# A cross-attention kernel: the context turned by VectorE, its keys and values made in four row tiles

## The chip, the cores and the metric

The kernel runs on one core of a Trainium2 chip. The metric is the device time of one execution in microseconds (us). The time before is the median of three runs.

## The reference

Two transformer layers on x (4 batches, 512 tokens, 320 channels), all in float32. Each layer is self-attention, cross-attention to a context (4 batches, 1601 tokens, 192 channels), and a gated feed-forward block with inner width 1280, each behind a layer norm and with a residual. Attention has 20 heads of 16 channels.

```python
h1 = _ln(x, n1_g, n1_b)
x = _attn(h1, h1, q1, k1, v1, o1_w, o1_b, heads) + x
h2 = _ln(x, n2_g, n2_b)
x = _attn(h2, context, q2, k2, v2, o2_w, o2_b, heads) + x
h3 = _ln(x, n3_g, n3_b)
a, g = jnp.split(h3 @ ff_w1 + ff_b1, 2, axis=-1)
x = a * gelu(g) @ ff_w2 + ff_b2 + x
```

`_attn` is softmax(q k^T / 4) v per head, then a projection. The same context serves both layers, with different weights.

## The kernel before

**Units and rounds.** The work is cut into units: for each layer, first self-attention, then cross-attention, over 4 batches and 5 groups of 4 heads (20 units each), then 4 feed-forward units. An attention unit (`main`, L883) walks over chunks of 128 keys: 4 chunks in self-attention, 13 in cross-attention, where the last one holds 65 keys. One chunk is a round. In a round TensorE makes the transposed scores of the chunk for the 4 heads (`st`, L891), ScalarE takes their exponentials (`pr`, L897), and one round later TensorE multiplies these with the values (`av`, L911). ScalarE copies `av` to `vo` (L927) and GpSimd adds it to the output (L928). Beside the scores of the current unit, TensorE computes the scores of the next unit the other way round (`sps`, L730 and L745), only for VectorE to find each query's maximum (L738, L755). The maxima are turned and sent by small DMAs on SP's queue into spare rows of q (`max_end`, L781), so that the score product itself subtracts them.

**Tiles of the array.** A head has 16 channels, so its q and k lie in a slot of 32 partitions, and a score product uses 32 rows of the array; two `st` and two `sps` products in different rows run together. `av` uses all 128 rows and 32 columns for each head. The projections for queries (`qps`, L601), keys (`kps`, L626), values (`vps`, L678) and output (`ops`, L839) have 96 to 128 rows and 32 columns, four products in different columns. Every product is in float32.

**Steps.** All the rest is done in steps, which stand in chains (L273): context, norm, queries and keys ("proj" and "early"), values, project, divide. `steps` (L343) is called once in a round, after the `av` product. It takes steps whose due time is next while a credit allows; the credit grows each round by what all queued steps cost over the time until they are due (`pace`, L321). Steps that cost nearly nothing (`LIGHT`, L276) are run two in a round. `until` (L368) runs a chain at once when its result is needed. The order of all instructions is thus fixed when the program is built.

**Banks.** There are eight PSUM banks in two rings of four: `ps_st` for `st` and `av`, `ps_m` for `sps`. A step takes one bank of `ps_m` (`step_bank`, L283).

**The context.** For each batch the context is loaded in pairs of chunks (`load_context`, L474) and turned on TensorE in seven steps (`turn`, L504): products with an identity matrix of up to 128 x 96 into one bank (`cps`, L514), copied by ScalarE (L518) to `ctxT`, which holds 96 partitions x 2 x 1601. The result is saved to memory for the second layer (L523), which loads it instead of turning it (L496). There is one `ctxT` buffer, which the feed-forward block uses too.

**Keys and values.** The keys of a group are made in four steps (`keys`, L621) of about 2 x 200 tokens: 2 parts of 96 channels x 4 products. ScalarE copies the bank to `kst`, and GpSimd spreads it over the slots of `kT` (`to_slots`, L541, L556: four instructions for a step). `kwhen` notes when each step's keys are there, and maxima of columns that are complete may start three half rounds later (`at_hand`, L1104). The values are made a chunk at a time (`values`, L669), in two parts of 8 and 12 heads (128 and 192 columns), and copied by ScalarE to `vals` (L686).

**Weights.** The deque `loads` is emptied by one entry in each attention unit. `load_cross` (L193) loads the weights of cross-attention, `load_ff` (L199) those of the feed-forward block, w1 in two DMAs of 1280 KB.

Of the kernel before, what the change touches and what calls it, by code (L numbers as in the profile page):

```python
# [36 lines left out]
CK = [(0, 0, 96), (1, 96, 96)]  # L37
NHC = FF // P
# [21 lines left out]
def kernel(ctx: ExitStack, tc: tile.TileContext, x, context, ws, out):  # L60
# [83 lines left out]
    wk2, wv2 = (wpool.tile([P, 2, D], F32, name=n) for n in ("wk2", "wv2"))  # L144
    w1 = wpool.tile([P, 2, 2 * FF], F32, name="w1")

# [46 lines left out]
    def load_cross(l):  # L193
        load_norm(l, 1)
        load_rows(wq2, ws[l]["q2"], DK)
        load_rows(wk2, ws[l]["k2"], CK)
        load_rows(wv2, ws[l]["v2"], CK)

    def load_ff(l):  # L199
# [11 lines left out]
        for k in FK:  # L211
            loads.append(lambda k=k: load_rows(w1, ws[l]["ff_w1"], [k]))
# [3 lines left out]


    class Unit:


        def __init__(self, l, kind, b, g):
            self.l, self.kind, self.b, self.g = l, kind, b, g
            self.cross = kind == "cross"
            self.nkeys = S2 if self.cross else N
            self.nch = (self.nkeys + P - 1) // P
            self.kck = CK if self.cross else DK

            s = slices(self.nkeys, 8 if self.cross else 2)
            self.kpairs = [s[i : i + 2] for i in range(0, len(s), 2)]
            self.kmade = 0  # L230
            self.kwhen = []
            self.vmade = [0, 0]
            self.made = {"q": 0, "k": 0}
            self.scored = 0
            self.valued = 0
            self.steps = 2 * self.nch if kind != "ff" else 2 * NHC + NQ
            self.before = self.other = None
            self.early = False
            self.own = {}
            self.pairs = self.hT = self.q = self.kvT = None  # L240
# [32 lines left out]
    chains = {n: deque() for n in ("divide", "project", "norm", "context", "early", "proj", "values")}  # L273
    clock = {"round": 0, "credit": 0.0, "lights": 0, "tiles": None}
# [68 lines left out]
    def steps(beside, lights=1):  # L343
# [3 lines left out]
        clock["lights"] = lights  # L347
        clock["tiles"] = True if beside is None else None
        done = 0
        while True:  # L350
# [13 lines left out]
            if cost == LIGHT:  # L364
                clock["lights"] -= 1
        clock["tiles"] = None
# [107 lines left out]
    def load_context(b, i):  # L474
# [9 lines left out]
        if rows % P:  # L484
            dma(out=t[: rows % P, full, :], in_=context[b, (c0 + full) * P : S2, :])
        ctx_in[b, i] = t


    saved = [dram.tile([CK[0][2], 2, S2], F32, name=f"ctxT{b}") for b in range(B)]

    def add_context(l, b, put, due, free):
        s = {}

        def load():
            s["cT"] = one.tile([P, 2, S2], F32, tag="ctxT", name="ctxT")
            dma(out=s["cT"][: CK[0][2]], in_=saved[b])  # L496
            s["round"] = clock["round"]

        if l:
            add("context", 0.0, load, due - 14, free)  # L500
            add("context", 0.0, lambda: put(s["cT"]), due - 2, yes, lambda: clock["round"] >= s["round"] + 8)
            return

        def turn(i):  # L504
            if i == 0:
                s["cT"] = one.tile([P, 2, S2], F32, tag="ctxT", name="ctxT")
            c0, n = CGRP[i]
            t = ctx_in.pop((b, i))
            rows = min(S2, (c0 + n) * P) - c0 * P
            ps = step_bank([P, 2, 2 * P], "cps")  # L510
            for k, at, w in CK:
                for c in range(n):
                    r = min(P, rows - c * P)
                    nc.tensor.transpose(  # L514
                        ps[:w, k, c * P : c * P + r], t[:r, c, at : at + w], ident[:r, :r]
                    )
            w = CK[0][2]
            nc.scalar.copy(s["cT"][:w, :, c0 * P : c0 * P + rows], ps[:w, :, :rows])  # L518
            if i + 2 < len(CGRP):
                load_context(b, i + 2)  # L520
            if i + 1 == len(CGRP):
                put(s["cT"])
                dma(out=saved[b], in_=s["cT"][:w])  # L523

        for i in range(len(CGRP)):
            add("context", 0.58, lambda i=i: turn(i), due - 2 * (len(CGRP) - i), free if i == 0 else yes)
# [31 lines left out]
    def add_proj(u):  # L558
        wq, wk = (wq2, wk2) if u.cross else (wq1, wk1)
        chain = "early" if u.early else "proj"  # L560

        due = lead(u) - 6

# [10 lines left out]
        if u.g == 0:  # L574
            last = units[u.before.i - u.before.g] if u.before else None

            def free():

                return last is None or last.made["k"] == G and last.vmade[1] == last.nch

            if u.cross and not u.early:
                add_context(u.l, u.b, lambda t: u.own.update(kv=t), due - 4, free)

            def hold():
                until(lambda: "h" in u.own, "norm")
                if u.cross:
                    until(lambda: "kv" in u.own, "context")
                u.hT = u.own["h"]
                u.kvT = u.own.get("kv", u.own["h"])

            add(chain, 0.0, hold, due - 4, yes, lambda: "h" in u.own and (not u.cross or "kv" in u.own))
# [29 lines left out]
        def keys(pair):  # L621
            ps = step_bank([P, 512], "kps")
            for k, at, n in u.kck:
                for i, to, gs in tiles:
                    c0, w = pair[i]
# [3 lines left out]
                        rhs=first.kvT[:n, k, c0 : c0 + w],  # L629
                        start=(k == 0),  # L630
                        stop=(k == len(u.kck) - 1),
                    )
            if u.i:
                stage = two.tile([P, N // 2], F32, tag="stage", name="kst")
                wide = min(w for _, w in pair)
                nc.scalar.copy(stage[:, :wide], ps[:, :wide])  # L636
            for i, (c0, w) in enumerate(pair):
                if u.i == 0:
                    to_slots(u.kT, u.k0 + c0, ps, w, i, True, keep)
                    continue  # L640
                if w > wide:
                    rows = slice(i * GD, (i + 1) * GD)
                    nc.scalar.copy(stage[rows, wide:w], ps[rows, wide:w])  # L643
                to_slots(u.kT, u.k0 + c0, stage, w, i, True)
            u.kmade += 1
            u.kwhen.append(-9 if start["on"] else clock["round"])
            first.made["k"] += u.kmade == len(u.kpairs)
# [5 lines left out]
        for part in range(parts):  # L653
            add(chain, (0.05 + 0.427 / parts,) * 3, lambda part=part: queries(part), due - 2, unread)
        for pair in u.kpairs:
            c0, w = pair[-1]
            chunks = (c0 + w + P - 1) // P

            def free(chunks=chunks):

                return u.other is None or u.other.scored >= min(chunks, u.other.nch)

            add(chain, (0.15 / len(u.kck) + w / 600,) * len(u.kck), lambda pair=pair: keys(pair), due + (c0 - w) // 300, free)

    def add_values(u):

        wv = wv2 if u.cross else wv1

        def values(i, cs):  # L669
# [3 lines left out]
            for c in cs:  # L673
                r = min(P, u.nkeys - c * P)
                at = (c - cs[0]) * w
                for k, _, n in u.kck:
                    for f, m in tiles_of(r):
                        nc.tensor.matmul(  # L678
                            ps[f : f + m, at : at + w],
                            lhsT=u.kvT[:n, k, c * P + f : c * P + f + m],  # L680
                            rhs=wv[:n, k, h0 * DH : h1 * DH],
                            start=(k == 0),
                            stop=(k == len(u.kck) - 1),
                        )
            m = len(cs)
            nc.scalar.copy(  # L686
                vals[:r, cs[0] : cs[0] + m, h0:h1, 0:DH],
                ps[:r, : m * w].rearrange("p (c h d) -> p c h d", c=m, d=DH),
            )
            u.vmade[i] += m  # L690

        for i, g in enumerate((0, 2)):
# [3 lines left out]
            whole = u.nkeys // P  # L696
            sets = [range(c, c + 1) for c in range(whole)]
            if u.nkeys % P:
                sets.append(range(whole, whole + 1))
            for cs in sets:  # L700

                def free(c=cs[-1], user=user):
                    return u.kvT is not None and (user is None or user.valued > min(c, user.nch - 1))

                add(
                    "values", (0.15 + w / 600 * len(u.kck),) * len(cs), lambda i=i, cs=cs: values(i, cs),
                    units[u.i + g].start + 2 * cs[0], free,
# [3 lines left out]
    def max_pairs(u):  # L711
# [7 lines left out]
        def have(end):  # L719
            assert keys_of(u) >= end  # L720

# [5 lines left out]
        def full_one(t, s, j):  # L727
            have((s + 1) * 512)
# [11 lines left out]
        def rest_two(heads):  # L740
            have(u.nkeys)
# [141 lines left out]
    def main(u, give, nxt):  # L883
# [3 lines left out]
        def score(c, j, pool=ps_st, tag="st"):  # L887
# [4 lines left out]
                st[:r, :], lhsT=u.kT[rows, u.k0 + c * P : u.k0 + c * P + r], rhs=u.q[rows, :], start=True, stop=True  # L892
# [172 lines left out]
    def before(u):  # L1065

        if u.kind == "cross" and u.g == 1 and u.b + 1 < B or u.kind == "self" and u.m == EARLY - 2:
            b = u.b + 1 if u.cross else 0
            if u.l == 0:
                load_context(b, 0)  # L1070
                load_context(b, 1)
        if u.kind == "self" and u.m == EARLY:

            add_context(u.l, 0, lambda t: units[u.i - u.m + B * G].own.update(kv=t), u.start + 36, yes)

    def after(u):

        stage[u.b] += 1
        if u.b == B - 1:
# [5 lines left out]
            if u.l + 1 < L:  # L1085
                if u.kind == "ff":
                    load_ff(u.l + 1)
                else:
                    load = load_self if u.kind == "self" else load_cross
                    loads.append(lambda: load(u.l + 1))  # L1090
# [4 lines left out]
    def columns(v, pairs):  # L1095

        full = v.nkeys // 512
        s = (full * NQ + bool(v.nkeys % 512) - len(pairs)) // NQ
        return min(v.nkeys, (s + 1) * 512)

    def keys_of(v):
# [143 lines left out]
```

## Time and profile before

| what | value |
|---|---|
| median of 3 runs | 3273.88 us (3269.45 to 3275.33) |
| the profiled execution, its own time | 3271.09 us |
| its span, first to last instruction | 3269.3 us |
| mean granted TensorE clock | 0.996 |
| TensorE, context keys (L626, 96 rows), busy | 135.7 us + 34.4 us for two forms, beside each other |
| VectorE, 512-column maxima (L738), 2560 of them, busy | 1591 us |
| ScalarE, exponentials (L897), busy | 1411.0 us |
| GpSimd, additions of `vo` (L928), 1277 ns each | 735.7 us |
| SP's DMA queue | 47.92 MB, 5.5% of 16 engines' span |

Busy time of a group is the time in which at least one of its instructions runs, so that the times of groups that run together must not be added. A float32 product stands as two records in the profile (two passes). A group's mean is that of one record with its latency, and is longer than the time from one start to the next. The timeline merges neighbouring instructions of one form into a line with its count.

### The profile page before, as it was taken

The page shows a single profiled execution, that of the slowest core. Times are in us where ns is not written, and L with a number is a line of the kernel's source. Part 1 is how long each engine was busy: PE and PEld are TensorE (multiplying, and loading weights), DVE is VectorE, ACT ScalarE, POOL GpSimd, SP SyncE. Part 2 cuts the span into 40 slices and gives each one's busy share as a digit, 9 for nine tenths or more (in the row PEclk, how much of TensorE's full clock was granted, in tenths as well). Part 3 has the DMA queues.
Part 4 walks back from the last instruction along what each step waited for, and adds up shares of the span by engine and source line. Part 5 has one row for each costly group of instructions (what it writes and reads, how often), then busy time and mean ns, then how long its engine had stood idle before and what let it go on. Part 6 is the DMA issues. An engine that isn't in the chain of part 4 may idle for free.

```text
span 3269.3 us, 82086 instructions
## 1 busy us (share of the span) xinstructions
PE 3221.7 (99%) x33554; PEld 1455.4 (45%) x33554; DVE 2090.6 (64%) x3844; ACT 2029.1 (62%) x4191; POOL 1525.4 (47%) x2254
## 2 busy tenths in 40 slices
PE   9999999999999999999999999999999999999999
PEld 4444444344444444355444444444444444443555
DVE  7777777677777777522248777777777777774221
ACT  4666467777877877711136665678778778775110
POOL 4545456556655655210224554566556556642000
PEclk9999999999999999999999999999999999999999
DMA  1210000100100000000002100000000000000000
GB/s 52 73 40 24 9 12 10 45 9 5 30 10 6 28 5 4 8 1 0 1 21 61 33 10 7 7 22 8 5 19 5 5 20 4 5 5 4 9 11 14
DMA packets 48844, 53.17 MB, mean 16 GB/s; under 512 B 23372, under 2 KB 41812, under 8 KB 47188
## 3 DMA queue, kind: packets, MB, share of 16 engines
q1 hardware_dynamic: 48384, 47.92, 5.5%
q8 instruction: 265, 4.34, 0.5%
q14 instruction: 111, 0.91, 0.1%
q0 software_dynamic: 64, 0.00, 0.0%
q10 hardware_dynamic: 20, 0.00, 0.0%
HBM read 29.21 MB, written 7.54 MB: 11 GB/s over the span
## 4 chain that ended last, share of the span: by engine, by line
PE 89%; DVE 5%; POOL 3%; issue 1%; ACT 1%; DMA 1%; SPq 1%; DVEq 0%; POOLq 0%; ACTq 0%
PE st L891 22%; PE av L911 19%; PE sps L730 15%; PE fps L1014 9%; PE yps L1049 5%; PE kps L626 4%; PE vps L678 4%; PE ops L839 3%; PE qps L601 3%; DVE nmax L738 2%; PE fps L1026 2%; PE sps L745 1%; PE hps L434 1%; DVE pm L738 1%; POOL kT L556 1%
## 5 line engine op out<-in xcount | busy, mean ns | idle before, releaser
L897 ACT ACTIVATE pr<-st 128x512 f32<-128x512 f32 (+1 forms) x2720 | 1411.0, 602 | 545.8 <-PE sps L730 425.8
L738 DVE TENSOR_REDUCE pm<-sps 128x1 f32<-128x512 f32 x1920 | 1195.1, 682 | 423.7 <-PE sps L730 420.9
L891 PE MATMUL st<-q,kT 32*128 32x512 f32 (+1 forms) x5440 | 1368.1, 617 | 21.7 <-ACT pr L897 6.9
L730 PE MATMUL sps<-kT,q 32*128 32x512 f32 x5120 | 1285.9, 620 | 3.8 <-ACT kst L643 2.4
L928 POOL TENSOR_TENSOR o<-o,vo 128x512 f32<-128x512 f32 x576 | 735.7, 1277 | 1048.1 <-ACT vo L927 882.1
L911 PE MATMUL av<-pr,vals 128*32 128x512 f32 (+1 forms) x5440 | 732.2, 607 | 4.8 <-ACT pr L897 4.8
L891 PEld LDWEIGHTS st<-q,kT 32*128 32x128 f32 (+1 forms) x5440 | 467.9, 181 | 333.6 <-ACT pr L897 160.4
L730 PEld LDWEIGHTS sps<-kT,q 32*128 32x128 f32 x5120 | 442.3, 184 | 231.6 <-issue 152.6
L738 DVE TENSOR_REDUCE nmax<-sps 128x1 f32<-128x512 f32 x640 | 395.9, 680 | 153.4 <-PE sps L730 151.8
L556 POOL TENSOR_SCALAR kT<-kst,keep,ones 64x200 f32<-64x200 f32 (+2 forms) x796 | 413.8, 520 | 80.0 <-ACT kst L636 22.3
L927 ACT COPY vo<-av 128x512 f32<-128x512 f32 x576 | 350.5, 609 | 19.9 <-PE av L911 19.2
L911 PEld LDWEIGHTS av<-pr,vals 128*32 128x32 f32 (+1 forms) x5440 | 110.1, 108 | 502.4 <-ACT pr L897 482.4
L1032 ACT ACTIVATE gl<-fps,b 128x512 f32<-128x512 f32 x80 | 54.8, 687 | 376.9 <-PE fps L1026 376.8
L1014 PE MATMUL fps<-hT,w 128*128 128x512 f32 x640 | 288.0, 599 | 0.0
L556 POOL TENSOR_SCALAR q<-qst,keep,zero 64x128 f32<-64x128 f32 (+1 forms) x476 | 229.8, 483 | 89.8 <-ACT qst L613 58.9
L1014 PEld LDWEIGHTS fps<-hT,w 128*128 128x128 f32 x640 | 117.4, 190 | 147.6 <-issue 141.9
L678 PEld LDWEIGHTS vps<-wv,ctxT 96*32 96x32 f32 (+1 forms) x3264 | 102.8, 109 | 108.0 <-issue 88.8
L678 PE MATMUL vps<-wv,ctxT 96*32 96x192 f32 (+2 forms) x3264 | 148.2, 299 | 0.0
L382 POOL TENSOR_SCALAR root<-root 128x4 f32<-128x4 f32 x23 | 5.3, 229 | 298.5 <-DVE root L376 297.9
L626 PE MATMUL kps<-ctxT,wk 96*32 96x200 f32 (+1 forms) x2560 | 135.9, 332 | 0.0
L1033 DVE SCALAR_TENSOR_TENSOR hid<-fps,b,gl 128x512 f32<-128x512 f32 x48 | 35.8, 750 | 152.5 <-ACT gl L1032 150.3
L601 PE MATMUL qps<-hT,wq 112*32 112x128 f32 (+3 forms) x2880 | 127.5, 309 | 4.3 <-DVE nmax L738 2.5
(79 smaller groups left out, 2244.2 us busy)
## 6 DMA issues: line engine op xcount, KB each, us to landing
aT<-o SPq DMA_DIRECT2D x320, 32.0 KB
q<-turned SPq DMA_DIRECT2D x636, 1.0 KB
ctxT<-ctxT SPq DMA_DIRECT2D x8, 1200.8 KB
w<-in_L_xattn_ff_w_dram SPq DMA_DIRECT2D x4, 1280.0 KB
ctxin<-in_ctx_dram SPq DMA_DIRECT2D x24, 192.0 KB
w<-in_L_xattn_ff_w_dram SPq DMA_DIRECT2D x4, 800.0 KB
out_dram<-x SPq DMA_DIRECT2D x16, 160.0 KB
x<-in_x_dram SPq DMA_DIRECT2D x3, 640.0 KB
```

What stands on the lines that cost most here:

```text
L556: nc.gpsimd.tensor_scalar(to, stage[rows, :w], keep[b][rows], more[rows], ALU.mult, ALU.add)
L601: nc.tensor.matmul(ps[to, :w], lhsT=wq[:n, k, gs], rhs=first.hT[:n, k, at[i] : at[i] + w], start=(k == 0), stop=(k == 2),)
L626: nc.tensor.matmul(ps[to, :w], lhsT=wk[:n, k, gs], rhs=first.kvT[:n, k, c0 : c0 + w], start=(k == 0), stop=(k == len(u.kck) - 1),)
L678: nc.tensor.matmul(ps[f : f + m, at : at + w], lhsT=u.kvT[:n, k, c * P + f : c * P + f + m], rhs=wv[:n, k, h0 * DH : h1 * DH], start=(k == 0),
L730: nc.tensor.matmul(ps, lhsT=u.q[j * SLOT : (j + 1) * SLOT, t * P : (t + 1) * P], rhs=u.kT[j * SLOT : (j + 1) * SLOT, u.k0 + s * 512 : u.k0 ...
L738: return lambda: nc.vector.tensor_reduce(to, ps, AX.X, ALU.max, negate=(ns == 1))
L891: nc.tensor.matmul(st[:r, :], lhsT=u.kT[rows, u.k0 + c * P : u.k0 + c * P + r], rhs=u.q[rows, :], start=True, stop=True)
L897: nc.scalar.activation(p[:r], st[:r], AF.Exp)
L911: nc.tensor.matmul(ps[i * SLOT : (i + 1) * SLOT, :], lhsT=columns_of[:r, head : head + SLOT], rhs=pr.pop((c, j))[:r, :], start=True, stop= ...
L927: nc.scalar.copy(vo, ps)
L928: nc.gpsimd.tensor_tensor(u.o, u.o, vo, ALU.add)
L1014: nc.tensor.matmul(ps, lhsT=w1[:, k, i * FF + c * P : i * FF + (c + 1) * P], rhs=u.hT[:, k, :], start=(k == 0), stop=False,)
```

## The change

The context is no longer turned as a whole. VectorE transposes it in blocks of 32 x 32: token t of chunk c lands on partition group t // 32, at column c x 32 + t % 32, with the 192 channels as 6 blocks of 32 on the 32 partitions. `ctxT` becomes 128 partitions x 6 x 416. So each of the four groups of 32 partitions holds its 32 tokens of every chunk, and the weights of keys and values are loaded four times, once for each group (`wk_q`, `wv_q`, in the space of w1, whose own load moves to the last unit of cross-attention). The last 65 tokens are turned on TensorE as well, for their values (`tail`).

A group's keys are made in one step: 6 channel blocks x 4 row groups x 2 halves of the columns, each product 32 rows x 64 columns of the array with 192 (or up to 224) moving columns, into four banks, two of each ring. ScalarE and VectorE copy two banks each; eight pieces then go to the slots, at most two in a round, in a chain of their own. The keys are due ten half rounds earlier, and maxima wait until all keys of the unit are there. In `kT` the columns now stand by row group (`cols`). Values are made for four chunks in one step: 6 channel blocks x 4 row groups, each product 32 rows x 128 columns. Self-attention keeps its steps.

```diff
+KB = CTX // 32
+QT = (NC2 - 1) * 32
+TAIL = S2 - 4 * QT
+HALF = QT // 2
...
+    w1_flat = w1.rearrange("p k f -> p (k f)")
+    wk_q, wv_q = (
+        w1_flat[:, i * KB * D : (i + 1) * KB * D].rearrange("p (k d) -> p k d", d=D) for i in range(2)
+    )
...
     def load_cross(l):
         load_norm(l, 1)
         load_rows(wq2, ws[l]["q2"], DK)
-        load_rows(wk2, ws[l]["k2"], CK)
         load_rows(wv2, ws[l]["v2"], CK)
+        for t, n in ((wk_q, "k2"), (wv_q, "v2")):
+            for i in range(4):
+                dma(out=t[i * 32 : (i + 1) * 32], in_=ws[l][n].rearrange("(k p) d -> p k d", p=32))
...
+    def load_first(l):
+
+        load_rows(w1, ws[l]["ff_w1"], FK)
...
-            ps = step_bank([P, 2, 2 * P], "cps")
-            for k, at, w in CK:
-                for c in range(n):
-                    r = min(P, rows - c * P)
-                    nc.tensor.transpose(
-                        ps[:w, k, c * P : c * P + r], t[:r, c, at : at + w], ident[:r, :r]
-                    )
-            w = CK[0][2]
-            nc.scalar.copy(s["cT"][:w, :, c0 * P : c0 * P + rows], ps[:w, :, :rows])
+            t, _ = ctx_in.pop((b, i))
+            for c in range(n):
+                at = (c0 + c) * 32
+                nc.vector.transpose(s["cT"][:, :, at : at + 32], t[:, c, :])
...
+        def tail():
+            ps = step_bank([P, 2, P], "cps")
+            for k, at, w in CK:
+                nc.tensor.transpose(ps[:w, k, :TAIL], s["last"][:TAIL, 0, at : at + w], ident[:TAIL, :TAIL])
+            w = CK[0][2]
+            nc.scalar.copy(s["tail"], ps[:w, :, :TAIL])
+            dma(out=saved_tail[b], in_=s["tail"])
+            put(s)
...
         for i in range(len(CGRP)):
-            add("context", 0.58, lambda i=i: turn(i), due - 2 * (len(CGRP) - i), free if i == 0 else yes)
+            add(
+                "context", LIGHT, lambda i=i: turn(i), due - 2 * (len(CGRP) - i), free if i == 0 else yes,
+                lambda i=i: clock["round"] >= ctx_in[b, i][1] + 3,
+            )
+        add("context", 0.3, tail, due)
...
+        keys_due = due - 10 if u.cross else due
...
+        def keys_of_context():
+
+            pss = quarter_banks("kps")
+
+            more = [max(0, min(32, TAIL - a * 32)) for a in range(4)]
+            for k in range(KB):
+                for a, ps in enumerate(pss):
+                    rows = slice(a * SLOT, (a + 1) * SLOT)
+                    for i in range(2):
+                        w = HALF + i * more[a]
+                        nc.tensor.matmul(
+                            ps[i * GD : (i + 1) * GD, :w],
+                            lhsT=wk_q[rows, k, u.g * GD : (u.g + 1) * GD],
+                            rhs=first.kvT[rows, k, i * HALF : i * HALF + w],
+                            start=(k == 0),
+                            stop=(k == KB - 1),
+                        )
+            stage = one.tile([P, 4, HALF + 32], F32, tag="kstage", name="kst4")
+            for a, ps in enumerate(pss):
+                copy = nc.vector.tensor_copy if a % 2 else nc.scalar.copy
+                copy(stage[:, a, :HALF], ps[:, :HALF])
+                if more[a]:
+                    copy(stage[GD:, a, HALF : HALF + more[a]], ps[GD:, HALF : HALF + more[a]])
+            for a in range(4):
+                for i in range(2):
+                    def piece(a=a, i=i):
+                        to_slots(u.kT, a * QT + i * HALF, stage[:, a, :], HALF, i, True)
+                        if i and more[a]:
+                            to_slots(u.kT, 4 * QT + a * 32, stage[:, a, HALF:], more[a], i, True)
+                        if a == 3 and i:
+                            there()
+
+                    u.kslots.append(piece)
...
+            add(chain, 2.45, keys_of_context, keys_due, free)
+            add_queries()
+            for i in range(8):
+                add(
+                    "slots", 0.0, lambda: u.kslots and u.kslots.popleft()(), keys_due,
+                    lambda: u.keyed, lambda: clock["slots"] > 0,
+                )
...
+    def quarter_banks(name):
+
+        return [
+            pool.tile([P, 512], F32, tag=tag, name=name) for pool, tag in ((ps_st, "st"), (ps_m, "m")) * 2
+        ]
...
+        def values_of_context(i, s):
+
+            h0, h1 = PARTS[i]
+            w = (h1 - h0) * DH
+            pss = quarter_banks("vps")
+            for k in range(KB):
+                for a, ps in enumerate(pss):
+                    rows = slice(a * SLOT, (a + 1) * SLOT)
+                    nc.tensor.matmul(
+                        ps[:, :w],
+                        lhsT=u.kvT[rows, k, s * P : (s + 1) * P],
+                        rhs=wv_q[rows, k, h0 * DH : h1 * DH],
+                        start=(k == 0),
+                        stop=(k == KB - 1),
+                    )
+            for a, ps in enumerate(pss):
+                copy = nc.vector.tensor_copy if a % 2 else nc.scalar.copy
+                copy(vals[:, 4 * s + a, h0:h1, 0:DH], ps[:, :w].rearrange("p (h d) -> p h d", d=DH))
+            u.vmade[i] += 4
...
+                    "values", 0.2 + w / 100, lambda i=i, s=s: values_of_context(i, s),
...
+        if u.kind == "cross" and u.m == B * G - 1:
+            load_first(u.l)
```

## The prediction

> **What bounds the kernel now.** I read the page first, then TensorE's timeline, then VectorE's timeline and its groups. The page (part 1) names the engine:
>
> ```profile
> span 3269.3 us, 82086 instructions
> PE 3221.7 (99%) x33554; PEld 1455.4 (45%) x33554; DVE 2090.6 (64%) x3844; ACT 2029.1 (62%) x4191; POOL 1525.4 (47%) x2254
> ```
>
> TensorE is busy 99% of the span, no other engine over 64%. So a step is worth what it adds to TensorE's round. I call one key chunk a round: four scores (`st`), four maxima products (`sps`), one `av`, then perhaps a step. TensorE's timeline of three rounds of the context attention (columns: start us, duration us, instruction, count):
>
> ```profile
> 2463.45 1.07 PE L911 MATMUL av<-pr,vals 128*32 128x512 f32 x8
> 2464.33 0.86 PE L626 MATMUL kps<-ctxT,wk 96*32 96x201 f32 x16
> 2465.13 0.70 PE L891 MATMUL st<-q,kT 32*128 32x512 f32 x2
> ...
> 2466.10 0.59 PE L891 MATMUL st<-q,kT 32*128 32x512 f32 x2
> ...
> 2466.53 0.59 PE L891 MATMUL st<-q,kT 32*128 32x512 f32 x2
> 2467.06 1.07 PE L911 MATMUL av<-pr,vals 128*32 128x512 f32 x8
> 2468.05 0.70 PE L891 MATMUL st<-q,kT 32*128 32x512 f32 x2
> ...
> 2469.98 1.07 PE L911 MATMUL av<-pr,vals 128*32 128x512 f32 x8
> ```
>
> From `av` to `av` the round with a key step lasts 3.61 us, the next one, without a step (a **bare round**), 2.92. The difference, 0.68 to 0.69 us, is the whole price of a key step. Two passes of scores start 0.43 us apart (2466.10, 2466.53): 512 columns on four strips of the array at once, 0.84 ns a column; each f32 product is two passes (5440 score records for 2720 exponentials).
>
> How close the others follow is in VectorE's timeline; in brackets is its idle time before:
>
> ```profile
> 2469.30 2.48 DVE L738 TENSOR_REDUCE pm<-sps 128x1 f32<-128x512 f32 x4 [0.44 <-PE sps L730]
> ```
>
> ```profile
> 683.64 0.70 DVE L809 STREAM_TRANSPOSE oturn<-o 128x512 f32<-128x512 f32 x1
> 684.37 0.25 DVE L811 RECIPROCAL rd<-oturn 128x16 f32<-128x16 f32 x1
> ...
> 687.22 0.41 DVE L815 TENSOR_TENSOR oturn<-oturn,rd 128x256 f32<-128x256 f32 x1
> 687.67 0.71 DVE L819 STREAM_TRANSPOSE o<-oturn 128x512 f32<-128x512 f32 x1
> 688.30 1.85 DVE L738 TENSOR_REDUCE pm<-sps 128x1 f32<-128x512 f32 x3
> ```
>
> In a bare round VectorE's four maxima take 2.48 us of 2.92 and leave 0.44. In the second fence a bare round (685.50 to 688.43 on TensorE) has 0.95 us of extra VectorE work before it and 1.12 after: the bare round still lasts 2.93, and the next, with a step, 3.69 where its kind lasts 3.36, so TensorE waited 0.32. From that: 0.95 + 1.12 less the spare 0.44 and 0.88 is a backlog of 0.75, of which about 0.42 us is hidden by the four banks and the rest is seen by TensorE. ScalarE in a bare round: 2.06 (four exponentials) + 0.62 = 2.68 of 2.92.
>
> **What the Trainium skill says.** "TensorEngine Tiling (Array Packing)", Tiling Modes: 32x128 gives four tiles, 32x64 eight, working independently, and a change of mode drains the engine. The trace agrees on four, and on the drain: `av` to a step of its own shape takes 0.88 us, to scores 0.99 to 1.00. It shows no 32x64 tile. "TensorE: Matmul & The Clock Gate", LDWEIGHTS: a load takes columns/1.2 ns, so 107 ns for 128 columns and 53 for 64 (estimates); the first score pass (2465.13 to 2465.66, 0.53) is 0.10 longer than the later ones, which agrees. "VectorE: DVE Perf Modes", The three transpose paths: VectorE turns 32x32 blocks only, hence the new layout; the groups show its price:
>
> ```profile
> L809 DVE STREAM_TRANSPOSE oturn<-o 128x512 f32<-128x512 f32 x80 | 56.0, 700 | 12.3 <-POOL o L928 12.2
> L785 DVE STREAM_TRANSPOSE turned<-nmax 128x32 f32<-128x32 f32 x80 | 16.8, 210 | 5.2 <-issue 1.5 <-DVE nmax L777 0.7
> ```
>
> **The change, part by part** (on the profiled execution: 3271.1 us, of which the span is 3269.3; it lies 2.8 under the median of the runs, 3273.9).
>
> *Keys.* Removed: 40 groups x 4 steps x 0.68 = 109 us. Added: 40 steps of 48 products. Eight tiles take 12 passes each; the widest moves 224 columns: 12 x 224 x 0.84 ns = 2.25 us, plus a drain 0.12 and a first load 0.05: 2.43, in all 97. Gain 12. Unknown: whether eight tiles run at once. From below nothing is left to gain (the widest tile's passes follow each other). From above, four at a time: 24 turns of about 200 columns, 4.0 us, a loss of 40 x 1.78 = 71. A limit on starting instructions would also show: the trace has pairs of load and product 27 ns apart (128-column query steps, 16 in 0.44 us), 96 of these make 2.6 us, a loss of 14. I take 2.43: `av`'s four column tiles stream from the same partitions at full rate.
>
> *Values.* A step of 192 columns is worth 3.58 - 2.92 = 0.65 us, one of 128 columns 3.36 - 2.92 = 0.44, by the same reading of their rounds. Eight batches x 12 chunks: 96 x (0.65 + 0.44) = 105. Added: 24 + 24 steps, 12 passes x 192 or 128 columns x 0.84 = 1.93 and 1.29: 77. They have the scores' shape, so no further drain. Gain 27; 107 ns loads behind 107 ns passes could cost 2 of it.
>
> *Context.* 24 of 28 transposing steps on TensorE go; a round with one lasts 3.50: 0.57 x 24 = 14. TensorE's sum is -53. The one long wait, 5.5 us for `ctxin` at 584 us, I leave in: the new order still puts such a load behind 15 weight loads on SP's queue. Now it is a VectorE transpose that waits for it; behind that stand the next maxima, and behind these the `sps` banks, so TensorE stops two score pairs later. ScalarE loses 28 copies of `ctxT` (0.59) and half of the key and value copies; it has no wait of its own to give back.
>
> *What is late next.* The same rounds with fewer steps: in the new instruction order 282 of the 520 rounds of the context attention are bare, 85 in the old (mostly one or two in a row). Each bare round has 0.44 us spare on VectorE, a round with a step 1.1 and more. So work that VectorE did under a step now shows. VectorE gets 52 transposes of 192 elements, 0.37 us each between the two rows above, 19 us; 40 x (2 x 0.35 + 0.18) = 35 us of key copies and 48 x 2 x 0.3 = 30 of value copies (between its 160-element add, 317 ns, and its 512-element copy, 691). The copies come just after a step of 1.3 to 2.4 us in which VectorE has run dry: hidden, and if that cover failed, 65 us. The transposes stand two to a round, with norm work, in a run of bare rounds: 0.75 to 1.7 us extra a round against 0.44. Following the backlog through the order by the rule above (TensorE waits for what exceeds 0.42), I get 13 us for the transposes, 10 for layer norm beside bare rounds, 10 for the divisions: 33.
>
> *Smaller.* Four banks are asked for at once, after four scores and four maxima that hold all eight; by the timelines the second maximum and third exponential are done 0.2 us before a step that follows `av`. After it, the second score pair wants banks 0.96 us after the step's end, and ScalarE's two copies and two slivers take 0.33 + 0.15 + 0.33 + 0.15 and some latency: 0.03 us a step, 3 in all. GpSimd: eight pieces two to a round, 4 x 0.51 us and slivers beside a 1.28 us addition, 3.3 to 3.9 of 2.92; it falls behind by up to 2.4 us, where a `vo` buffer comes round after about 3: 2 us. SP: eight weight loads instead of two in `load_cross` and 1.28 MB of w1 at the last context unit of each layer, a unit (about 46 us) ahead of its reader; the q rows issued behind a reload of the context waited 2.0 us twice already: 4. Together 9.
>
> Sum: -53 + 33 + 9 = -11: 3260, and a little for the profiled run's place under the median: **3261**.
>
> **Rivals.** *Bare rounds hold* (3233): VectorE's extra work falls beside steps more often than I counted, 38 of the 53 arrive. For it: bare runs are short. Against: the 0.32 us wait shown above. *VectorE becomes the bound* (3290): the rival on the other side. Place: runs of bare rounds. Of 84 us more on VectorE, half of the copies show besides what I counted: 30 us more. It decides from a total of waits of 53 us, where the gain is gone; measured slower from about 60. *Eight tiles don't run at once* (3331): keys 4.2 us a step, 71 lost. Against: the column tiles of `av` and row tiles of the scores each reach full rate alone.
>
> **Chances.** Forecast 0.58 (own range 3240 to 3282), bare rounds hold 0.17, VectorE bound 0.15, tiles apart 0.10. Within the forecast 0.36 is faster by over 0.2% (what a measurement of this kernel can tell), 0.16 within, 0.06 slower; with the others (VectorE's rival gives 0.02 to within and 0.13 to slower): faster 0.53, same 0.18, slower 0.29. The range, 3225 to 3300, reaches over the first rival and VectorE's; the last is left out.
>
> **What would show it.** Key steps of 48 products with 2.4 us more than a bare round; value steps 1.9 and 1.3; bare rounds of 2.92 us and others lengthened with VectorE named as releaser; VectorE busy about 2170 us; no transposes of `ctxin` on TensorE but the tail's. A key step near 4 us, or waits for VectorE well over 45 us, would prove me wrong.

## The result: slower, and the profile after

| | before | after |
|---|---|---|
| median | 3271.66 us (3268.83 to 3275.33) | 3353.06 us (3351.61 to 3357.68) |
| ratio, 95% interval | | 1.0251 [1.0233, 1.0268] |
| span of the profiled execution | 3269.3 us | 3350.4 us |

The forecast of 3261 us and its range, 3225 to 3300, both missed: instead of a gain of 11 us there is a loss of 81. Part 1 of the page of the kernel after:

```profile
span 3350.4 us, 83401 instructions
PE 3262.8 (97%) x33970; PEld 1506.1 (45%) x33970; DVE 2165.8 (65%) x4112; ACT 1989.1 (59%) x4031; POOL 1608.9 (48%) x2498
```

VectorE's 2165.8 us are what I forecast (about 2170). TensorE's share fell from 99% to 97%, and GpSimd is busy 84 us longer at a share of only 48%. In the chain that ended last, TensorE falls from 89% to 80% of the span, GpSimd rises from 3% to 9%. The view of waits (engine, line, releaser: us in total, times, longest) says who waits:

```profile
PEld st L995 <- ACT pr L1001: 365.5, 491, 3.6
ACT pr L1001 <- POOL o L1032: 166.2, 117, 5.9
```

In the kernel before, the same two are less than half and less than a fifth as long:

```profile
PEld st L891 <- ACT pr L897: 160.4, 360, 2.2
ACT pr L897 <- POOL o L928: 29.7, 31, 2.6
```

TensorE's scores wait for exponentials, and these for GpSimd's additions of `vo`. An exponential's result needs a buffer of the ring of eight that `vo` uses too (`prs`). While GpSimd has not added an older `vo`, its buffer isn't free.

First the step that I forecast in most detail. The timeline of one key step and its round (start us, duration us, instruction, count):

```profile
2606.52 1.07 PE L1015 MATMUL av<-pr,vals 128*32 128x512 f32 x8
2607.51 2.50 PE L697 MATMUL kps<-ctxT,w 32*64 32x192 f32 x96
...
2609.95 0.70 PE L995 MATMUL st<-q,kT 32*128 32x512 f32 x2
...
2610.04 0.32 ACT L707 COPY kst<-kps 128x192 f32<-128x192 f32 x1 [1.75 <-PE kps L697]
...
2610.38 0.18 ACT L709 COPY kst<-kps 64x32 f32<-64x32 f32 x1
...
2610.92 0.16 ACT L709 COPY kst<-kps 64x1 f32<-64x1 f32 x1
...
2611.13 0.75 PE L835 MATMUL sps<-kT,q 32*128 32x512 f32 x2
...
2612.24 1.07 PE L1015 MATMUL av<-pr,vals 128*32 128x512 f32 x8
```

From the step's first product to the first score: 2609.95 - 2607.51 = 2.44 us; the median over the key steps that scores follow directly is 2.43, as forecast. All eight tiles ran at once. But the round, from `av` to `av`, is 5.72 us long here and 5.75 in the median, 2.83 more than a bare one. The other 0.40 lies after the step: ScalarE's four copies take from 2610.04 to 2611.08, 1.13 us after the first score, and VectorE's end 0.06 us later. The second pair of maxima products, which starts 0.96 us after the first score in a bare round, finds its banks in use and starts at 1.18; the fourth score likewise.

Now the additions. Rounds of another group (GpSimd's lines, the waiting exponentials, and `av` as the mark of a round):

```profile
2564.38 1.06 PE L1015 MATMUL av<-pr,vals 128*32 128x512 f32 x8
2564.62 3.15 POOL L587 TENSOR_SCALAR kT<-kst,keep,ones 64x192 f32<-64x192 f32 x6
...
2567.43 1.06 PE L1015 MATMUL av<-pr,vals 128*32 128x512 f32 x8
2567.85 1.28 POOL L1032 TENSOR_TENSOR o<-o,vo 128x512 f32<-128x512 f32 x1
2569.12 3.09 POOL L587 TENSOR_SCALAR kT<-kst,keep,ones 64x192 f32<-64x192 f32 x6
...
2575.78 1.06 PE L1015 MATMUL av<-pr,vals 128*32 128x512 f32 x8
2575.88 2.06 POOL L587 TENSOR_SCALAR q<-qst,keep,zero 64x128 f32<-64x128 f32 x4
2578.02 1.26 POOL L1032 TENSOR_TENSOR o<-o,vo 128x512 f32<-128x512 f32 x1
2579.32 0.60 ACT L1001 ACTIVATE pr<-st 128x512 f32<-128x512 f32 x1 [3.17 <-POOL o L1032]
...
2581.69 1.94 PE L1015 MATMUL av<-pr,vals 128*32 128x512 f32 x8
...
2586.18 1.07 PE L1015 MATMUL av<-pr,vals 128*32 128x512 f32 x8
```

Two pieces with a narrow rest are six instructions and 3.15 us; with an addition, 4.43 us in a round of 2.93. GpSimd falls behind by 1.5 us a round, then come the query pieces, 2.06. ScalarE stands still for 3.17 us, and the round from 2575.78 to 2581.69 takes 5.91 us. The next takes 4.49 although no wait explains that: `av` lasts 1.94 instead of 1.06. There the clock records show TensorE at half speed for 3.41 us.

### The profile page after: what moved, and what is told of

The parts are those of the page before. It is cut to its first block, busy times and chain, and to the rows that moved or that the text cites. A ratio compares the mean times of both kernels' runs of the same rounds, so it can differ in the third digit from the quotient of the medians.

```text
span 3350.4 us, 83401 instructions
## 1 busy us (share of the span) xinstructions
PE 3262.8 (97%) x33970; PEld 1506.1 (45%) x33970; DVE 2165.8 (65%) x4112; ACT 1989.1 (59%) x4031; POOL 1608.9 (48%) x2498
## 4 chain that ended last, share of the span: by engine, by line
PE 80%; POOL 9%; DVE 5%; issue 2%; ACT 2%; SPq 1%; DMA 1%; POOLq 0%; DVEq 0%; ACTq 0%
PE st L995 21%; PE av L1015 16%; PE sps L835 11%; PE fps L1118 8%; PE yps L1153 5%; POOL kT L587 4%; POOL o L1032 3%; PE ops L943 3%; PE kps L697 3%; PE vps L788 3%; PE qps L639 2%; PE fps L1130 2%; DVE nmax L843 2%; DVE pm L843 2%; POOL q L587 1%
## 5 line engine op out<-in xcount | busy, mean ns | idle before, releaser
L995 PE MATMUL st<-q,kT 32*128 32x512 f32 (+1 forms) x5440 | 1421.8, 620 | 56.2 <-ACT pr L1001 42.8
L835 PE MATMUL sps<-kT,q 32*128 32x512 f32 x5120 | 1351.1, 627 | 14.9 <-POOL kT L587 9.3
L995 PEld LDWEIGHTS st<-q,kT 32*128 32x128 f32 (+1 forms) x5440 | 525.4, 181 | 599.2 <-ACT pr L1001 365.5
L1015 PE MATMUL av<-pr,vals 128*32 128x512 f32 (+1 forms) x5440 | 742.6, 615 | 2.0 <-ACT pr L1001 2.0
L587 POOL TENSOR_SCALAR kT<-kst,keep,ones 64x192 f32<-64x192 f32 (+3 forms) x1036 | 496.0, 479 | 158.1 <-ACT kst L707 64.7
L943 PEld LDWEIGHTS ops<-wo,aT 112*32 112x32 f32 (+1 forms) x3072 | 98.1, 110 | 67.5 <-issue 52.7
L639 PEld LDWEIGHTS qps<-hT,wq 112*32 112x32 f32 (+1 forms) x2880 | 87.5, 113 | 90.7 <-issue 47.6
L465 POOL TENSOR_TENSOR x<-x,brow 128x320 f32<-128x320 f32 x96 | 83.4, 886 | 91.4 <-DVE hn L439 79.3
```

Of the source, the lines that this page charges most:

```text
L587: nc.gpsimd.tensor_scalar(to, stage[rows, :w], keep[b][rows], more[rows], ALU.mult, ALU.add)
L639: nc.tensor.matmul(ps[to, :w], lhsT=wq[:n, k, gs], rhs=first.hT[:n, k, at[i] : at[i] + w], start=(k == 0), stop=(k == 2),)
L835: nc.tensor.matmul(ps, lhsT=u.q[j * SLOT : (j + 1) * SLOT, t * P : (t + 1) * P], rhs=u.kT[j * SLOT : (j + 1) * SLOT, u.k0 + s * 512 : u.k0 ...
L943: nc.tensor.matmul(ps[f : f + m, : D // 2], lhsT=aT[:n, k, t * P + f : t * P + f + m], rhs=wo[:n, k, cols], start=(k == 0), stop=(k == 2),)
L995: nc.tensor.matmul(st[:r, :], lhsT=u.kT[rows, u.k0 + u.cols[c] : u.k0 + u.cols[c] + r], rhs=u.q[rows, :], start=True, stop=True)
L1015: nc.tensor.matmul(ps[i * SLOT : (i + 1) * SLOT, :], lhsT=columns_of[:r, head : head + SLOT], rhs=pr.pop((c, j))[:r, :], start=True, stop= ...
```

## The experiments

Each ratio is to the kernel before on the same chip. "The wait for additions" is what the view of waits gives for ScalarE's exponentials and copies of `vo` that wait for `o`: 166.2 us in the kernel after and 29.7 in the kernel before. The expectations of e5, e10 and e12 count by another sum, which is somewhat larger (189 us for the kernel after). A wait "follows" query pieces when the unbroken stretch of GpSimd's work that ends with the addition (no pause over 0.2 us) holds some; in the kernel after that is 104 of the 166 us, and 56 follow key pieces alone.

**e1: larger pieces, one a round.** Two row groups in one instruction, so 12 GpSimd instructions a group instead of 22. TensorE's order stays.

```diff
-        clock["lights"], clock["slots"] = lights, 2
+        clock["lights"], clock["slots"] = lights, 1
...
+                to = u.kT[b * GD : (b + 1) * GD, : 4 * QT].rearrange("p (a w) -> p a w", w=QT)
+                nc.gpsimd.tensor_scalar(
+                    to[:, a : a + 2, i * HALF : (i + 1) * HALF], stage[rows, a : a + 2, :HALF],
```

> The changed kernel, whose key pieces go to the slots in fewer and wider GpSimd instructions: two row groups at once (64 x 384 instead of two of 64 x 192) and the two slivers of 32 columns together, 12 instructions a group instead of 22, about 6.9 us instead of 10.2; half as many pieces, one a round, so TensorE's order stays. Theory (GpSimd falls behind, ScalarE waits for the vo buffer, TensorE for ScalarE): ScalarE's wait for GpSimd's addition, 166 us in the changed kernel, falls below 70, and the time falls by 50 to 90 us, to 3265 to 3300. Rival (VectorE's backlog in bare rounds): nothing that VectorE does is changed, the time stays within 10 us of 3353. Rival (four banks handed over at once): the same, no change.

3314.47 us, ratio 1.0141 [1.0122, 1.016]: 39 us less than the kernel after. The wait in the view of waits:

```profile
ACT pr L1012 <- POOL o L1043: 99.7, 73, 4.3
```

The wait fell by 66 us, but less than forecast, and the time stayed above the forecast range. Of what is left, 84 us follow query pieces.

**e2: nine buffers.** `prs` with `bufs=9`.

> The changed kernel with nine instead of eight buffers in the ring that holds the exponentials and vo; nothing else differs. Theory (GpSimd's addition frees the vo buffer late): each buffer comes round one allocation, about 0.5 us, later, so of 117 waits of ScalarE for GpSimd (166 us, 1.4 us each) some 0.4 us each goes: 30 to 60 us less waiting, the time falls by 20 to 50 us. Rival (VectorE's backlog) and rival (banks): no change, within 10 us of 3353.

3337.19 us, ratio 1.0207 [1.0187, 1.0226]: 16 us less. The wait moved to the copy of `vo` (108.9 us), which now asks for the buffer first. More slack helps, but does not cure.

**e3: keys in half products.** All channel blocks but the first are split into two products, 176 records a step instead of 96; the columns moved are the same.

```diff
-                        nc.tensor.matmul(
+                        for f, t in ((0, HALF // 2), (HALF // 2, w)) if k else ((0, w),):
+                            nc.tensor.matmul(
```

> The changed kernel, whose key products (32 rows x 64 columns, 192 to 224 moving columns) are issued as two of about 96 and 96 to 128 columns from the second channel block on: 88 products instead of 48 a group, the same columns moved. Key steps took 2.83 us in the changed kernel where 2.43 was forecast. Theory (pairs of weight load and product start no faster than about 27.7 ns): 176 pairs take 4.9 us and a key step about 5.0 us, 2.2 us x 40 = 87 us more in all. Rival (the widest tile's columns or a slower stream set the step): the step stays at 2.8 us, or grows by less than 0.5 us, with less than 20 us in all.

3397.61 us, ratio 1.0392 [1.0369, 1.0415]. The step itself took 3.32 us instead of 2.43, and the wait after it nearly vanished (key round 6.30 us against 5.75). The expectation took the round's 2.83 us for the step; the step was 2.43. Neither theory's number came: 176 records in 3.32 us are 19 ns apart, so there is no limit at 27 ns, but short passes aren't free either. Ten more passes per tile cost 0.89 us, 89 ns each. What sets this is left open. So is a part of the loss: 0.55 us in 40 rounds are 22 of the 45 us that e3 loses to the kernel after, while half of the key rounds grew by more than that, up to 3.2 us.

**e4: context turned twice.** VectorE issues each of the 52 transposes of `ctxin` a second time.

> The changed kernel with each of VectorE's 52 context transposes issued twice; 19 us more work for VectorE, in the bare rounds ahead of a new batch of the first layer. Theory (VectorE was not the cause; it waits less often than GpSimd): at most 10 us slower. Rival (VectorE's backlog in bare rounds is the bound): 19 us or more slower, and waits for VectorE's maxima on TensorE grow in the first layer's cross-attention.

3363.38 us, ratio 1.0286 [1.0266, 1.0305]: 10 us more for 20 us of VectorE's work. That agrees in size with my forecast of 13 us for the transposes, and stands at the edge of the theory's 10. VectorE's transposes aren't the main cause.

**e5: pieces and queries apart.** As e1, and a query step is not taken in a round that has a piece.

```diff
-                add(chain, (0.05 + 0.427 / parts,) * 3, lambda part=part: queries(part), due - 2, unread)
+                add(
+                    chain, (0.05 + 0.427 / parts,) * 3, lambda part=part: queries(part), due - 2, unread,
+                    lambda: not u.cross or clock["slots"] > 0,
+                )
...
-            clock["slots"] -= name == "slots"
+            clock["slots"] -= name in ("slots", "proj")
```

> As e1 (pieces of two row groups, one piece a round), and in addition a query step is not issued in a round that has a key piece, so that GpSimd never gets both in one round. In e1, 63 of the 112 us that ScalarE stood still just ahead of the end of an addition followed a stretch of GpSimd that held q pieces. Theory (GpSimd's bursts make the additions late): these waits fall from about 100 us to under 40, and the time from 3314 to 3275-3295. Rival (what is left in e1 is VectorE's extra work and the banks, GpSimd only reports it): the time stays within 8 us of e1, 3306-3322, and waits for VectorE take the place.

3273.79 us, ratio 1.0004 [0.9993, 1.0014], just under the theory's range. The wait for additions is 46.8 us. The whole loss is gone with TensorE's and VectorE's work as it was; only the order of TensorE's steps moved, and e12 below has this order too. GpSimd's timeline of one group's pieces:

```profile
2500.33 1.27 POOL L1046 TENSOR_TENSOR o<-o,vo 128x512 f32<-128x512 f32 x1 [7.35 <-ACT vo L1045]
2501.59 1.41 POOL L716 TENSOR_SCALAR kT<-kst,keep,ones 64x384 f32<-64x384 f32 x2
2503.32 1.26 POOL L1046 TENSOR_TENSOR o<-o,vo 128x512 f32<-128x512 f32 x1 [0.32 <-ACT vo L1045]
2504.57 1.42 POOL L716 TENSOR_SCALAR kT<-kst,keep,ones 64x384 f32<-64x384 f32 x2
2506.32 1.27 POOL L1046 TENSOR_TENSOR o<-o,vo 128x512 f32<-128x512 f32 x1 [0.34 <-ACT vo L1045]
```

A piece and an addition take 2.7 us, and GpSimd waits for the next `vo` instead of being late for it.

**e6: e5 with nine buffers.**

> As e5 with a ring of nine buffers instead of eight for exponentials and vo. Theory: a vo buffer comes round later, so the additions that are still late no longer hold the exponentials: 5 to 15 us under e5, 3265-3285, which would be near the kernel before (3267 to 3272). Rival (the ring matters only while GpSimd has bursts): within 4 us of e5.

3268.81 us, ratio 0.9993 [0.9984, 1.0003]; the wait is 16.4 us. The gain over e5 is within the intervals: not shown.

**e7 and e8: short additions.** In cross-attention only 64 of the 512 columns of `vo` are added, in the kernel after (e7) and in the kernel before (e8).

```diff
-                nc.gpsimd.tensor_tensor(u.o, u.o, vo, ALU.add)
+                w = 64 if u.cross else N
+                nc.gpsimd.tensor_tensor(u.o[:, :w], u.o[:, :w], vo[:, :w], ALU.add)
```

> The changed kernel with only the first 64 of 512 columns of vo added in cross-attention; the rest of each sum is left out. Every other instruction and their order stay. An addition then takes about 0.35 us instead of 1.28, so the pieces and an addition fit into a bare round. Theory (most of the loss is GpSimd's): the time falls by at least 70 us, to 3250-3285, and half-clock windows of TensorE fall from 17 to under 9. Rival (VectorE's additional work and the four banks at once make the loss): it falls by less than 35, and stays above 3318.

> The same short additions in the kernel before: only the first 64 of 512 columns of vo are added in cross-attention, the rest of each sum is left out. A control for e7: the kernel before shows 29.7 us of ScalarE's waits for additions, most of which it does not pass on; both theories expect a gain of 0 to 15 us, 3253-3272. If it gains as much as e7 does, the additions are simply too long in both kernels, and the change did not make GpSimd the limit.

e7: 3253.55 us, ratio 0.9947 [0.9932, 0.9962], 99.5 us less than the kernel after. e8: 3267.73 us, ratio 0.9992 [0.9985, 0.9999], 2.4 less than the kernel before beside it. The stretches at half clock fell from 17 to 6. So GpSimd's part in the loss is about 97 us, and without it the change gains 3267.73 - 3253.55 = 14 us. It may be somewhat more: e7 still has 46.5 us of the wait, all after query pieces, and e8 has 18.1. The clock is part of it. Spans and mean granted clocks of the kernel after and of e7:

```profile
core 0: 3350.4 us, clock 0.988
```

```profile
core 0: 3251.3 us, clock 0.995
```

0.012 x 3350 = 40 us of full speed were not granted in the kernel after, 16 in e7 and 13 in the kernel before. So up to some 24 of the 99.5 us are half clock, most of which follows standstills of TensorE (last section).

**e9: whole copies.** As e6; both halves of the columns move up to 224, and a bank is copied in one instruction.

```diff
-                        w = HALF + i * more[a]
+                        w = HALF + more[a]
...
-                copy(stage[:, a, :HALF], ps[:, :HALF])
-                if more[a]:
-                    copy(stage[GD:, a, HALF : HALF + more[a]], ps[GD:, HALF : HALF + more[a]])
+                copy(stage[:, a, : HALF + more[a]], ps[:, : HALF + more[a]])
```

> As e6, and the three narrow copies of a key step (the up to 32 extra columns of half the partitions: 0.18 and 0.15 us on ScalarE, 0.19 on VectorE) become part of the wide ones; the products of the other half move the extra columns too, beside tiles that are as wide already, so the step on TensorE stays at 2.43 us. Theory (the round after a key step is 0.40 us longer since its exponentials and maxima start only when four copies are through, at 1.13 and 1.22 us): the copies end about 0.35 us earlier and the key round falls from 5.73-5.75 us to 5.35-5.50; 8 to 14 us in all, 3253-3262. Rival (the longer round comes from the four banks being asked for at once, whatever the copies take): the key round stays above 5.65 and the time within 4 us of e6.

3260.14 us, ratio 0.9959 [0.9943, 0.9974]: faster than both kernels and, with intervals apart, than e6. A key round of its timeline:

```profile
2492.93 1.07 PE L1027 MATMUL av<-pr,vals 128*32 128x512 f32 x8
...
2493.93 2.50 PE L697 MATMUL kps<-ctxT,w 32*64 32x224 f32 x96
2496.46 0.57 ACT L707 COPY kst<-kps 128x224 f32<-128x224 f32 x2 [1.76 <-PE kps L697]
...
2498.35 1.07 PE L1027 MATMUL av<-pr,vals 128*32 128x512 f32 x8
```

The copies take 0.57 us instead of 1.04. The key round's median is 5.42 us, and the step still 2.43. So the length of the copies made most of the longer round (0.31 of 0.40 us), not the four banks as such. One thing in the expectation was misread: exponentials start some 1.16 us after the first score in a bare round as well (two passes come first). What was late were the last score and the last maxima products.

**e10: five even pieces.** As e9, with four pieces of one instruction (64 x 768) and a fifth with the narrow rest.

> As e9, with GpSimd's pieces evened out: four pieces of one instruction each (64 partitions, four row groups, 768 elements, an estimated 0.99 us from 0.50 for 192 and 0.665 for 384), and a fifth with the narrow rest (1.5 us), so that no piece with an addition exceeds a bare round of 2.93. Theory (GpSimd's bursts are what is left of its loss): 0 to 6 us under e9, 3249-3260, and waits of ScalarE just ahead of an addition's end under 12 us (20 in e6). Rival (a longer single instruction delays the addition behind it more): 0 to 5 us over e9.

3270.68 us, ratio 0.9989 [0.9983, 0.9996]: worse than e9, though the wait fell from 17.2 to 5.0 us as the theory wanted. The rival had the direction, but its 0 to 5 us are too few, and a late addition is not the reason. What I see instead, without a run that tests it alone: a fifth piece makes a unit's keys complete a round later, and maxima wait for all of them; counted by their records, 49 rounds carry none or half of their maxima (41 in e9), and 13 carry 22 records or more instead of 8 (8 such in e9).

**e11: small pieces, spread.** The kernel after with one small piece a round and queries apart: eight rounds of pieces instead of four.

> The changed kernel with its eight small pieces and ring of eight, only spread: one piece a round, and no query step in a round with a piece. GpSimd's total work stays that of the changed kernel, about 1609 us. TensorE's steps shift: about 40 more rounds of 678 are without a step, since query steps come later. It tells bunching from amount. Bunching: 3270-3295, near e5. Amount (22 instructions a group are too many however they are spread): above 3315.

3479.27 us, ratio 1.0636 [1.0618, 1.0655], neither theory's number. The wait for additions is 18.5 us: the spreading did its work with GpSimd as busy as before (1615 us). The likely reason is that the keys came too late, which no run tests alone: 72 rounds have no maxima (32 in the kernel after), 46 only half (2), and 49 carry 22 records or more (5). So e11 can't tell bunching from amount by its time.

**e12: queries apart alone.** The kernel after, small pieces two a round, queries apart; TensorE's steps in the order of e5.

> The changed kernel with its eight small pieces, two in a round as before, ring of eight; only the query steps are kept out of rounds with pieces. TensorE's steps stand in the order of e5, the maxima as early as there, so e11's late maxima are avoided; GpSimd's total work stays about 1609 us. Of the 189 us that ScalarE stood just ahead of an addition's end in the changed kernel, 83 followed a stretch with q pieces, 57 one with key pieces alone. Bunching (what counts is GpSimd's work in neighbouring rounds): these waits fall to 90-130 us and the time to 3300-3325, between the changed kernel and e5. Amount (what counts is the sum of small instructions): it stays above 3335, and e5's gain is that of the merging.

3339.21 us, ratio 1.021 [1.0193, 1.0227]: 14 us less than the kernel after, in the rival's range. The wait for additions rose to 194.0 us; 140 of it follow key pieces alone, 56 in the kernel after. The gain is no larger than what the clock gave back: 24 us of full speed were not granted, 40 in the kernel after.

Round by round TensorE does the same in e12 as in e5, so the 65 us between the two come from how the key pieces are cut. What counts is whether GpSimd's work fits the four rounds of pieces. Small pieces and additions need about 3 x 4.4 + 3.5 = 17 us of the 11.7 that four bare rounds last. The backlog is still there when the queries come, so keeping them out gains little. Merged pieces and additions need about 12.7 in e5: three rounds fit, and only the last, with the narrow rest, is too long (4.6 us). Then keeping the queries out gains the 41 us from e1 to e5.

## Why the prediction was wrong, step by step

| step | forecast | what the runs show |
|---|---|---|
| keys on TensorE | -12, 2.43 us a step | -12, 2.43 us a step |
| values | -27, steps of 1.93 and 1.29 | -22, 2.09 and 1.35 |
| context off TensorE | -14 | taken as forecast: no such steps left but the tail's |
| round after a key step (banks and copies) | +3 (0.03 a step) | +15 (0.37 to 0.40 a step) |
| VectorE, SP and the rest | +37 | about +19 (not measured: what remains of the -14 from e8 to e7) |
| GpSimd | +2 | +97 (e7 against e8) |

**The step that failed** is "GpSimd: eight pieces two to a round ... it falls behind by up to 2.4 us, where a `vo` buffer comes round after about 3: 2 us". Three things are wrong in it. I took 3.3 to 3.9 us for a round's pieces and addition; it is 4.4 where rests come with them. Two rests of 32 columns cost 0.74 us, where 3.9 leaves less than 0.6 for them, and the gaps of about 0.08 us between the instructions, 0.4 in such a round, I left out. Four rounds then leave a backlog of 17 - 11.7 = 5 us, not 2.4, and that is more than the 3 us after which, by my estimate, a `vo` buffer comes round. I followed the backlog through the pieces alone and left out the query pieces, 2.06 us twice, in the rounds just after or beside them. And I priced a late addition at little more than nothing, while each one stops exponentials and scores, and half clock often follows. e1, e5, e7 and e12 show the cause from four sides.

**Key copies.** The step "ScalarE's two copies and two slivers take 0.33 + 0.15 + 0.33 + 0.15 and some latency: 0.03 us a step" had the durations and the time at which banks are wanted (0.96 us) right. But the copies begin 0.09 us after the first score and end at 1.13, VectorE's at about 1.2, so banks come 0.2 to 0.3 us late, which grows to 0.40 by the end of the round. e9 shortened the copies and got 0.31 us a round back (5.73 in e6).

**Right.** Eight tiles run at once: the rival of 3331 us came near the measured time for a reason that did not occur. TensorE's own saving is about 48 us against 53. VectorE did not become the bound: its busy time was as forecast, and TensorE's waits for maxima ahead of scores, 7.0 and 4.8 us in all, are near those of before (4.7 and 5.0). SP's price of 4 us did not show: the scores waited 1.4 us for q rows, 5.2 before. The long wait for `ctxin` stayed, as left in: 6.7 us on VectorE, and behind it 5.3 us on TensorE in one wait for a maximum, where TensorE waited 5.5 before. Bare rounds are 2.92 us where nothing waits.

GpSimd stood at 47% of the span, and that average hid it. In the rounds where its work was bunched it had more to do than a round is long; I had the prices of its instructions to see most of that.

## What to carry to other kernels

When a change gathers work into fewer steps, sum every engine's work over the few rounds in which it now falls, including what others put there, and set it against those rounds' length; the engine's share of the span can hide it. A buffer ring that two engines share ties the fast one to the slow one: ask who returns the buffer last. Small instructions on GpSimd cost mostly their fixed part (0.34 of 0.50 us for 192 columns here), so merge them before spreading them, and check who waits for the last one.

## What the runs showed of the hardware

**GpSimd's price.** Groups of the kernel after (busy us, mean ns of one):

```profile
L587 POOL TENSOR_SCALAR kT<-kst,keep,ones 64x192 f32<-64x192 f32 x640 | 321.9, 503 | 105.3 <-ACT kst L707 64.7
L587 POOL TENSOR_SCALAR kT<-kst,keep,ones 64x32 f32<-64x32 f32 x160 | 59.6, 372 | 13.4
L587 POOL TENSOR_SCALAR kT<-kst,keep,ones 64x1 f32<-64x1 f32 x80 | 27.6, 346 | 6.3
```

With 384 columns it is 665 ns (e1), with 768 columns 990 ns (e10): 0.34 us and 0.84 ns a column. The page "GPSIMD Engine Reference" of the Trainium skill, section 3.1, gives 1.03 cycles an element for its simplest loops and reckons with 1.2 GHz, from which I estimate 0.86 ns, and the traces agree; it speaks of a dispatch for each instruction without a figure for GpSimd. Here that fixed part is 22 x 0.34 = 7.5 of some 10 us a group.

**Half clock after short standstills.** The clock records of the kernel after hold 17 stretches at half speed, each 3.41 us or a small multiple (one cut by the end), those of the kernel before 5. Three of the 17 follow gaps of TensorE of 4.6 to 5.3 us. Ahead of 13 others it stood still for 40 to 73% of the 3.41 us before, in one gap of 1.4 to 2.7 us. "TensorE: Matmul & The Clock Gate" of the Trainium skill, section HAM oscillation, asks for no gaps over about 3.4 us; here shorter ones were followed by half clock too. But not always: one such window with 44% of standstill in the kernel after, and one with 52% in e12, were not. And two of the stretches of the kernel before follow windows with only 5 and 6%; I can't say why.

**Eight tiles of 32 x 64** took 96 records in 2.43 us, at the full rate of each tile. Each tile's passes of 224 columns start 189 ns apart, which is 0.84 ns a column as in the scores, so no time for weight loads shows. With passes half as long (e3) this rate is not reached.
